# Placing tokens' rows by expert in memory, and gathering the experts' results by token

## The chip, the cores and the metric

The kernel runs on one core of one Trainium2 chip. The metric is the device time of one execution in microseconds (us); kernels are compared by the median of several executions. The engines are called as the profile calls them: PE (matrix multiply; PEld is its weight load), DVE (vector), ACT (activations), POOL (GpSimd, which also issues the indirect DMAs) and SP (which issues the plain DMAs).

## The reference

All data are float32. `x` is 32 x 112 x 256 (batch, time, feature), the context is 32 x 375 x 256. One decoder layer is computed: a delta-rule attention block, a cross-attention with 16 heads over the context, and a mixture of six experts. Only the last matters for the change:

```python
xt = layernorm(x).reshape(-1, 256)
logits = xt @ gate_w.T + gate_b
w, idx = top_k(sigmoid(logits), 2)            # two of six experts for each token
w = w / (w.sum(-1, keepdims=True) + 1e-8)
ge = sum(one_hot(idx, 6) * w[..., None], 1)
y = 0
for e in range(6):
    h = silu(xt @ ew1[e].T) * (xt @ ew3[e].T)
    y = y + ge[:, e:e+1] * (h @ ew2[e].T)
z = (silu(xt @ fc1.T) * (xt @ fc2.T)) @ fc3.T # shared by all tokens
x = x + y + z
```

## The kernel before

The 32 batches are worked in 8 groups of `GB` = 4 batches (448 tokens; a tile is 112 tokens by 4 batches by 256 features, 448 KB). The loop runs over 128 quads of cross-attention work (a batch, half of the heads, and so on) and two slots more. Sixteen slots make one group, about 146 us. The cross-attention of one group is the backbone; into its slots the loop puts pieces of other streams: `main` (the delta block of the next group), `kv` (keys and values of the next batch), and `others` (`mixture_sparse`, the mixture of the group before).

**Order of the work.** A `Recorder` collects all instructions as nodes with modelled prices and dependences, and `flush` writes out the order on PE, DVE and ACT. POOL's and SP's instructions stand in their queues in the order that this plan gives them; each of the two queues then runs in order. All recorded operations carry one line in the profile, L376, but for those written by functions of their own (the experts' matmuls `up` at L1329 and `down` at L1346, the results' scatter at L1357). A DMA's arrival is modelled in the plan, and on the chip each instruction waits by semaphores for what it really needs.

**The mixture.** The tokens of the first seven groups (`SB` = 28 batches, 3136 tokens) are routed sparsely: each token goes to its two experts, 6272 rows in all, done in `NTM` = 54 tiles of `TM` = 128 rows. The last group's tokens pass through all six experts (`mixture_dense`).

- `normed` makes `a3`, the normalised tokens of a group, in a ring of three buffers (tag `h`), which the delta block's tiles use too.
- `dispatch` (L1099) stores `a3` plainly to `rows` by SP, works out with DVE and two small matmuls a place for each token and choice (`row_i`: expert times `CAP` plus the count so far, where `free` holds the next free place of each expert), and issues eight indirect scatters on POOL, one for each batch and choice. Each writes 112 numbers of 4 bytes, the token's number, to that place of one of eight `lists`. The lists are zeroed at the start by eight DMAs on POOL.
- `mixture_sparse` ends by keeping the group's residual and shared part in memory (`kept<-x`).
- `tables` (L1202), in the last group, works out from the counts which expert each tile has (`which`), gathers the eight lists for the 54 tiles by eight indirect gathers, adds and turns them by eight matmuls against the identity (`plist`), and so gets `take` (which row of `rows` each slot of a tile takes) and `put` (where in `results` its result goes; a spare row for an empty slot).
- `gather` and `sparse_tiles` (L1294, L1302) work a pipeline over the tiles: an indirect gather of 128 rows (POOL), a transpose (PE, ACT), `up`, silu and product (ACT, DVE), a transpose, `down`, a copy to `y`, and an indirect scatter of `y` into `results` (POOL).
- `combine` (L1384) runs beside the dense experts of the last group. For each of the seven groups it loads `kept` and the two halves of `results` plainly by SP, into nine borrowed tiles (`homes`, so three groups are in flight), and DVE adds both halves with their gates (56 operations); `store` writes the group out.

At the start SP's queue holds the loads of inputs and weights, then the writes and reads by which the delta block turns its blocks (`blocks<-W`, `C<-blocks`, `X<-blocks`). In a middle group SP's queue holds the loads of context (`cT`) and mask (`mk`), the row store, `kept`, and the load of x two groups ahead.

Of the kernel before, what the change touches and what calls it, by code (L numbers as in the profile page):

```python
# [88 lines left out]
class Recorder:  # L89
# [135 lines left out]

    def together(self, cost):

        rec = self

        class Piece:  # L230
            def __enter__(self):
                rec.whole, rec.held = cost, None

            def __exit__(self, *_):
                rec.whole = rec.held = None

        return Piece()
# [143 lines left out]
def tile_decoder(ctx: ExitStack, tc: tile.TileContext, t: dict, out: bass.AP):  # L381
# [24 lines left out]
    CAP = NL * TM  # L406
# [16 lines left out]

    lists = [dram.tile([NE * CAP, 1], F32, name=f"lists_{i}") for i in range(2 * GB)]
    rows = dram.tile([SB * T, D], F32, name="rows")

    results = dram.tile([2 * SB * T + NTM * TM, D], F32, name="results")
# [19 lines left out]
    while s < T:  # L449
# [27 lines left out]
    zeros = att.tile([TM, NE * NL], F32, tag="neg", name="zeros")  # L477
    nc.vector.memset(zeros, 0.0)
# [9 lines left out]
    )  # L488
    number = const.tile([T, 2, SB], F32, tag="number", name="number")
    nc.gpsimd.iota(  # L490
        number, pattern=[[SB * T, 2], [T, SB]], base=1, channel_multiplier=1, allow_small_or_imprecise_dtypes=True
# [25 lines left out]
    for table in lists:  # L517
        nc.gpsimd.dma_start(out=table.rearrange("(p l) o -> p (l o)", p=TM), in_=zeros)
# [10 lines left out]
    def matmul(dst, lhsT, rhs, start=True, stop=True):  # L529
        n = 1  # L530
        for k in dst.shape[1:]:
            n *= k
        spent[0] += 2 * max(0.125, 0.017 + n / 1200)
        nc.tensor.matmul(dst, lhsT, rhs, start=start, stop=stop)
# [5 lines left out]
    def bank(name):  # L540
        return rec.bank()
# [557 lines left out]
    def dispatch(g, a3, place, ge):  # L1099

        nc.sync.dma_start(
            out=rows[g * GB * T : (g + 1) * GB * T].rearrange("(b t) d -> t b d", t=T), in_=a3
        )
# [23 lines left out]
        for b in range(GB):  # L1127
            for c in range(2):
                i = g * GB + b
                nc.gpsimd.indirect_dma_start(  # L1130
                    out=lists[2 * b + c][:], out_offset=bass.IndirectOffsetOnAxis(ap=row_i[:, c, i : i + 1], axis=0),
                    in_=number[:, c, i : i + 1], in_offset=None,
                )
            if b < GB - 1:
                yield

# [65 lines left out]
    def tables():  # L1202


        def tab(name, shape, dt=F32):
            return late.tile(shape, dt, tag=name, name=name)
# [4 lines left out]
        at = tab("at", [1, NTM])  # L1211
        nc.gpsimd.iota(at, pattern=[[1, NTM]], base=0, channel_multiplier=0, allow_small_or_imprecise_dtypes=True)
        line = tab("line", [NTM, 1])
        nc.gpsimd.iota(line, pattern=[[0, 1]], base=0, channel_multiplier=1, allow_small_or_imprecise_dtypes=True)
# [4 lines left out]
        more = scratch[:, : NE * NL].rearrange("p (e l) -> p e l", l=NL)  # L1219
# [7 lines left out]
        for e in range(1, NE):  # L1227
# [4 lines left out]
        nc.vector.tensor_tensor(d, off[:, 1:], off[:, : NE - 1], ALU.subtract)  # L1232

        past = tab("tpast", [NTM, NE - 1])
        nc.vector.tensor_scalar(past, before_e[:NTM, 1:], line, None, ALU.is_le)
        nc.vector.tensor_tensor(past, past, d[:NTM], ALU.mult)
        src = tab("tsrc", [NTM, 1])
        nc.vector.tensor_reduce(out=src, in_=past, axis=AX.X, op=ALU.add)
        nc.vector.scalar_tensor_tensor(src, src, 1.0 / TM, line, ALU.mult, ALU.add)
        nc.vector.tensor_scalar_min(src, src, float(NE * NL - 1))  # L1240
        srci = tab("tsrci", [NTM, 1], U32)
        nc.vector.tensor_copy(srci, src)

        shape = [1, NTM, NE - 1]
        over = scratch[:1, NE * NL : NE * NL + NTM * (NE - 1)].rearrange("p (i e) -> p i e", e=NE - 1)
        nc.vector.tensor_tensor(
            over, at[:1].unsqueeze(2).to_broadcast(shape), before_e[:1, 1:].unsqueeze(1).to_broadcast(shape), ALU.is_ge
        )
        expert = tab("expert", [1, NTM])
        nc.vector.tensor_reduce(out=expert, in_=over, axis=AX.X, op=ALU.add)  # L1250
        which = tab("which", [1, NTM], I32)
        nc.vector.tensor_copy(which, expert)
        yield
        listed = []
        for i, table in enumerate(lists):
            part = late.tile([NTM, TM], F32, tag=("xg", "xg", "xg", "xg", "xT", "xT", "hs", "hs")[i],
                             name=f"listed_{i}", bufs=4 if i < 4 else 2 if i < 6 else 3)
            nc.gpsimd.indirect_dma_start(
                out=part, out_offset=None, in_=table.rearrange("(l p) o -> l (p o)", p=TM),
                in_offset=bass.IndirectOffsetOnAxis(ap=srci, axis=0),  # L1260
            )
            listed.append(part)
            if i % 2 == 1:
                yield
        pt = bank("plist")
        for i, part in enumerate(listed):
            matmul(
                pt[:, :NTM], part, ident[:NTM, :NTM], start=(i == 0), stop=(i == len(listed) - 1)
            )
        num = tab("num", [P, NTM])  # L1270
        nc.vector.tensor_scalar_add(num, pt[:, :NTM], -1.0)
        taken = tab("ttaken", [P, NTM])
        nc.vector.tensor_scalar(taken, num, 0.0, None, ALU.is_ge)
        second = tab("tsecond", [P, NTM])
        nc.vector.tensor_scalar(second, num, float(SB * T), -float(SB * T), ALU.is_ge, ALU.mult)
        nc.vector.tensor_tensor(second, second, num, ALU.add)
        nc.vector.tensor_scalar_max(second, second, 0.0)
        take = tab("take", [P, NTM], U32)
        nc.vector.tensor_copy(take, second)
        spare = tab("spare", [P, NTM])  # L1280
        nc.gpsimd.iota(
            spare, pattern=[[TM, NTM]], base=2 * SB * T, channel_multiplier=1, allow_small_or_imprecise_dtypes=True
        )
        nc.vector.tensor_tensor(num, num, spare, ALU.subtract)
        nc.vector.tensor_tensor(num, num, taken, ALU.mult)
        nc.vector.tensor_tensor(num, num, spare, ALU.add)
        put = tab("put", [P, NTM], U32)
        nc.vector.tensor_copy(put, num)
# [3 lines left out]
        yield from sparse_tiles(take, put, which, gathers)  # L1292
# [9 lines left out]
    def sparse_tiles(take, put, which, xgs):  # L1302
# [4 lines left out]
        xTs, hs, hTs, at, scatters = {}, {}, {}, {}, []  # L1307
# [33 lines left out]
        def down(i):  # L1341
            p, hT = bank("pw2"), hTs[i]

            def issue():
                for c in range(CH):
                    rec.nc.tensor.matmul(  # L1346
                        p[:, :D].real(), hT[:, c, :], w2[:, bass.ds(at[i] * (CH * D) + c * D, D)],
                        start=(c == 0), stop=(c == CH - 1),
                    )

            rec.add("tensor", "down", [p], [hT, ew2], (issue, (), {}), cost=1.0)
            spent[0] += 1.0
            y = late.tile([TM, D], F32, tag="y", name=f"y_{i}", bufs=3)
            nc.vector.tensor_copy(y, p[:, :D])

            def scatter():
                sent = rec.nc.gpsimd.indirect_dma_start(  # L1357
                    out=results[:], out_offset=bass.IndirectOffsetOnAxis(ap=put[:, i : i + 1], axis=0),
                    in_=y, in_offset=None,
                )  # L1360
                for other in scatters:
                    tc.declare_no_dep(sent.ins, other.ins, reason="they write different rows")
                scatters.append(sent)

            rec.add(
                "gpsimd", "indirect_dma_start", [results[:]], [y, put[:, i : i + 1]], (scatter, (), {}), loose=True
            )
# [16 lines left out]
    def combine():  # L1384
# [7 lines left out]
        def ask(g):  # L1392
            three = []
            for i in range(3):
                h = homes[(3 * g + i) % len(homes)]
                if i == 0:
                    src = kept[g].rearrange("b t d -> t b d")
                else:
                    at = ((i - 1) * SB + g * GB) * T
                    src = results[at : at + GB * T].rearrange("(b t) d -> t b d", t=T)  # L1400
                nc.sync.dma_start(out=h, in_=src)
                three.append(h)
            return three
# [70 lines left out]
    for n in range(len(quads) + 2):  # L1474
# [29 lines left out]
        if last:  # L1504
            mains.append(main)
            side += [others] * ((0, 0, 0, 1, 1, 1, 2, 1, 1, 1, 1, 0, 0, 0, 0, 0)[i] if g < groups else 0)
            side += [tiles] * ((0, 0, 0, 0, 0, 0, 0, 1, 1, 1, 1, 1, 3, 4, 4, 4)[i] if g < groups else 3)
        else:
            if g > 0 and i in (3, 4, 5, 7, 8, 9, 10, 11, 12):
                side.append(others)  # L1510
            if i == 13 and g + 2 < groups:
                x_of[g + 2] = load_x(g + 2)
                following = ahead(g + 2)
# [116 lines left out]
```

## Time and profile before

| what | value |
|---|---|
| median of 17 runs | 1458.04 us (1453.1 to 1463.65) |
| profiled execution, its time | 1454.55 us |
| its span | 1452.9 us, 26668 instructions |
| granted PE clock, mean | 0.972 |
| DMA | 73.13 MB in 77170 packets, 29864 of them under 512 B |
| HBM | read 51.12 MB, written 20.28 MB |

Profile times are microseconds from the span's start. A line of the timeline gives start, duration, engine, line, operation, what is written from what is read, and in brackets the idle time of the engine before it and what ended it; "issue" is a wait that the profile does not explain, "remote" one that it cannot place. SPq is SP's DMA queue.

The work by time: startup to about 100 us, the middle to about 1140 (seven groups), tables and lists to 1196, the tile phase to T0 = 1380.1, the dense experts with `combine` to the end.

```profile
PE   6679999999999899999999999999989889999998
DMA  8100100101010101010101020102015111222283
...
L376 POOL DMA_INDIRECT lists<-number,row_i x56 | 52.8, 944 | 110.5 <-DVE tn L376 57.0
L376 POOL DMA_INDIRECT xg<-rows,take x54 | 52.5, 972 | 73.2 <-PE bank L376 56.2
...
L1357 POOL DMA_INDIRECT results<-y,put x54 | 53.2, 985 | 39.6 <-DVE y L376 20.1
```

The first two rows are busy tenths in 40 slices of the span (PE, DMA engines). The others give count, busy time, mean ns of one and idle time before.

### The profile page before, as it was taken

Reading aid. Unit: us, or ns where it says so; the run is one execution under the profiler, and the core shown is the slowest. Engines: PE = TensorE matmul, PEld = TensorE weight load, DVE = VectorE, ACT = ScalarE, POOL = GpSimd, SP = SyncE. Lnnn points to the kernel's source line nnn. Section 1 sums busy time; section 2 is a strip of 40 time slices with the busy share of each in tenths; the row PEclk is TensorE's granted clock in tenths of the full one; section 3 lists DMA queues with packets and bytes.
Section 4 is the critical chain, followed back from the end, with each engine's and each line's share of the span. In section 5 each row is a group of like instructions: output and inputs, shape, how many; then the busy total and the mean of one; then the engine's idle time right before and its main releaser. Section 6 shows DMA issues by size and latency. Waiting matters only on the chain.

```text
span 1452.9 us, 26668 instructions
## 1 busy us (share of the span) xinstructions
PE 1376.8 (95%) x9716; PEld 932.5 (64%) x9716; DVE 965.0 (66%) x3164; ACT 701.3 (48%) x1946; POOL 319.7 (22%) x492
## 2 busy tenths in 40 slices
PE   6679999999999899999999999999989889999998
PEld 4456766766676567766766676667656565656655
DVE  6545766866785578667857786778548555455577
ACT  2123756654665356546655555456548364222110
POOL 3122000320032003200320032003200314556500
PEclk9779999999999999999999999999999889999999
DMA  8100100101010101010101020102015111222283
GB/s 232 26 7 13 34 16 17 48 17 42 17 48 16 42 16 48 17 42 16 48 17 42 16 49 16 42 16 59 6 48 154 20 43 58 90 82 88 68 234 101
DMA packets 77170, 73.13 MB, mean 50 GB/s; under 512 B 29864, under 2 KB 72808, under 8 KB 77040
## 3 DMA queue, kind: packets, MB, share of 16 engines
q1 hardware_dynamic: 69296, 56.00, 14.1%
q0 software_dynamic: 7744, 15.43, 3.6%
q8 instruction: 77, 1.26, 0.4%
q14 instruction: 53, 0.43, 0.1%
HBM read 51.12 MB, written 20.28 MB: 49 GB/s over the span
## 4 chain that ended last, share of the span: by engine, by line
PE 74%; DVE 11%; ACT 4%; issue 3%; DMA 2%; POOL 2%; another core or an unknown queue 1%; DVEq 0%; SPq 0%; ACTq 0%
PE bank L376 64%; PE bank L1329 7%; PE bank L1346 3%; ACT e L376 2%; POOL W L376 2%; DVE e L376 2%; DVE rs_u L376 2%; DVE x L376 1%; DMA blocks<-W 1%; DVE W L376 1%; ACT eT L376 1%; DVE rs_i L376 1%; DVE vx L376 1%; DMA X<-blocks 1%
## 5 line engine op out<-in xcount | busy, mean ns | idle before, releaser
L376 ACT ACTIVATE e<-e,nmx 112x375 f32<-112x375 f32 x512 | 306.2, 603 | 172.4 <-DVE nmx L376 169.7
L376 DVE CUSTOM_DVE_ANT_0 e<-bank,neg,flip 112x375 f32<-112x375 f32 x512 | 282.4, 604 | 42.1 <-PE bank L376 29.7
L376 ACT COPY eT<-bank 125x448 f32<-125x448 f32 x384 | 184.9, 530 | 117.8 <-PE bank L376 78.4
L376 PEld LDWEIGHTS bank<-ident,e 112*125 112x125 f32 x1536 | 187.4, 189 | 39.9 <-issue 15.6
L376 PE MATMUL bank<-ident,e 112*125 112x112 f32 x1536 | 205.0, 277 | 7.8 <-issue 3.0
L376 PE MATMUL bank<-kx,qz 32*112 32x375 f32 x1024 | 125.8, 526 | 0.0
L376 PE MATMUL bank<-eT,vx 125*32 125x112 f32 x3072 | 105.0, 265 | 17.6 <-ACT eT L376 10.5
L376 PEld LDWEIGHTS bank<-eT,vx 125*32 125x32 f32 x3072 | 70.3, 110 | 70.3 <-issue 46.9
L1329 PE MATMUL bank<-ew,xT 128*128 x216 | 104.0, 605 | 2.4 <-ACT xT L376 2.3
L376 PE MATMUL bank<-w_xwvT,cT 128*125 128x256 f32 x384 | 104.2, 399 | 0.0
L376 PE MATMUL bank<-cT,w_xwkT 128*128 128x375 f32 x256 | 96.4, 502 | 2.5 <-ACT eT L376 2.5
L376 ACT ACTIVATION_READ_ACCUMULATOR e<-e,nmx 112x1 f32 x512 | 97.8, 191 | 0.0
L376 DVE SCALAR_TENSOR_TENSOR hs<-hs,bank 128x256 f32<-128x256 f32 x108 | 45.4, 421 | 77.2 <-ACT hs L376 65.0
L376 DVE SCALAR_TENSOR_TENSOR qk<-qk,bank 128x448 f32<-128x448 f32 x56 | 34.8, 621 | 81.7 <-ACT qk L376 54.2
L376 ACT ACTIVATE hs<-bank 128x256 f32<-128x256 f32 x54 | 20.7, 384 | 119.5 <-PE bank L1329 99.1
L376 PEld LDWEIGHTS bank<-w_xwvT,cT 128*125 128x125 f32 x384 | 68.3, 191 | 14.0 <-issue 6.0
L376 POOL DMA_INDIRECT lists<-number,row_i x56 | 52.8, 944 | 110.5 <-DVE tn L376 57.0
L376 PEld LDWEIGHTS bank<-kx,qz 32*112 32x112 f32 x1024 | 44.0, 172 | 41.1 <-issue 13.3
L376 PEld LDWEIGHTS bank<-cT,w_xwkT 128*128 128x128 f32 x256 | 44.9, 193 | 38.1 <-issue 9.8
L376 POOL DMA_INDIRECT xg<-rows,take x54 | 52.5, 972 | 73.2 <-PE bank L376 56.2
L376 POOL TENSOR_TENSOR u<-h,nwb 112x1024 f32<-112x1024 f32 x7 | 16.6, 2370 | 232.3 <-issue 218.8
L1357 POOL DMA_INDIRECT results<-y,put x54 | 53.2, 985 | 39.6 <-DVE y L376 20.1
(251 smaller groups left out, 2394.0 us busy)
## 6 DMA issues: line engine op xcount, KB each, us to landing
cT<-in_ctxT_dram SPq DMA_DIRECT2D x32, 375.0 KB
mk<-in_mask_dram SPq DMA_DIRECT2D x32, 164.1 KB
x<-in_x_dram SPq DMA_DIRECT2D x7, 448.0 KB
rows<-h SPq DMA_DIRECT2D x7, 448.0 KB
kept<-x SPq DMA_DIRECT2D x7, 448.0 KB
e<-results SPq DMA_DIRECT2D x6, 448.0 KB
eT<-results SPq DMA_DIRECT2D x4, 448.0 KB
out_dram<-x SPq DMA_DIRECT2D x4, 448.0 KB
```

The source lines that it names most:

```text
L376: getattr(getattr(self.nc, name), op)(*[real(a) for a in args], **{k: real(v) for k, v in kwargs.items()})
L1329: rec.nc.tensor.matmul(p.real(), xT[:, c, :], w13[:, bass.ds(at[i] * (NC * 2 * MI) + c * 2 * MI, 2 * MI)], start=(c == 0), stop=(c == NC - 1),
L1346: rec.nc.tensor.matmul(p[:, :D].real(), hT[:, c, :], w2[:, bass.ds(at[i] * (CH * D) + c * D, D)], start=(c == 0), stop=(c == CH - 1),)
L1357: sent = rec.nc.gpsimd.indirect_dma_start(out=results[:], out_offset=bass.IndirectOffsetOnAxis(ap=put[:, i : i + 1], axis=0), in_=y, in_of ...
```

## The change

`rows` becomes a memory of `NE * CAP` rows by expert and place (`CAP` is now 3136, as many as there are tokens), with one row of zeros after the last. `dispatch` no longer stores `a3` plainly. It scatters the rows of `a3` themselves (112 rows of 1 KB) to their two places, eight indirect DMAs on POOL for each group as before. The lists, the numbers and the lists' zeroing are gone. Places that may stay empty must hold zeros: the loop issues `clear_places(g, e)` on SP, one store of 448 KB of zeros from `blank` for each of the first seven groups and six experts (42 in all), in slots 8 to 13 of a group; a clear covers the places of expert e that lie from g*448 on. `hold` ties the node just recorded to the last PE node before it, which is the plan's means of keeping clears and scatters near the place where they are recorded. In SP's queue of the changed program the clears stand in seven places: seven of them near the start (behind the loads of weights and a mask, ahead of a context and of `blocks<-W` and `C<-blocks`), six in each of five middle groups (ahead of `cT`, `kept<-x`, `mk` and `x<-in_x_dram`), and five beside the last scatters. In the middle groups their waits interleave with the scatters: two scatters, clears, two scatters, and so on.

`tables` computes `take` by DVE from the counts alone (tile times 128 plus place, shifted by each expert's offset, and the row of zeros where a tile ends beyond its expert's tokens), with no list gathers and no matmuls, and rewrites `row_i` to say where in `results` each token's two results lie. `sparse_tiles` stores each `y` plainly by SP, 128 KB a tile, to its own 128 rows of `results`. `combine` gets both halves by eight indirect gathers of 112 rows for each group on POOL, 56 in all; `kept` is still loaded by SP. The first piece of `tables` is asked for in slot 10 of the last group, before in slot 7.

In the order of the last group's POOL queue stand now: eight scatters, 54 gathers of rows, 56 gathers of results.

```diff
+    def hold(self):
+
+        so_far = next(node for node in reversed(self.nodes) if node.eng == "PE")
+        self.nodes[-1].before[so_far.at] = so_far
...
-    CAP = NL * TM
+    CAP = SB * T
...
-    lists = [dram.tile([NE * CAP, 1], F32, name=f"lists_{i}") for i in range(2 * GB)]
-    rows = dram.tile([SB * T, D], F32, name="rows")
-    results = dram.tile([2 * SB * T + NTM * TM, D], F32, name="results")
+    ZERO = NE * CAP
+    rows = dram.tile([ZERO + 1, D], F32, name="rows")
+    results = dram.tile([NTM * TM, D], F32, name="results")
+    blank = const.tile([T, D], F32, tag="blank", name="blank")
+    nc.vector.memset(blank, 0.0)
...
-    for table in lists:
-        nc.gpsimd.dma_start(out=table.rearrange("(p l) o -> p (l o)", p=TM), in_=zeros)
+    nc.gpsimd.dma_start(out=rows[ZERO : ZERO + 1], in_=blank[:1])
...
     def dispatch(g, a3, place, ge):
-        nc.sync.dma_start(
-            out=rows[g * GB * T : (g + 1) * GB * T].rearrange("(b t) d -> t b d", t=T), in_=a3
-        )
...
-                i = g * GB + b
-                nc.gpsimd.indirect_dma_start(
-                    out=lists[2 * b + c][:], out_offset=bass.IndirectOffsetOnAxis(ap=row_i[:, c, i : i + 1], axis=0),
-                    in_=number[:, c, i : i + 1], in_offset=None,
-                )
+                place_row(g * GB + b, c, a3[:, b, :])
...
+    def clear_places(g, e):
+        some = rows[e * CAP + g * GB * T : e * CAP + (g + 1) * GB * T]
+        nc.sync.dma_start(
+            out=some.rearrange("(t r) d -> t r d", t=T), in_=blank.unsqueeze(1).to_broadcast([T, GB, D])
+        )
+        rec.hold()
+    placed = []
+    def place_row(i, c, row):
+        where = row_i[:, c, i : i + 1]
+        def scatter():
+            sent = rec.nc.gpsimd.indirect_dma_start(
+                out=rows[:], out_offset=bass.IndirectOffsetOnAxis(ap=where, axis=0), in_=row, in_offset=None
+            )
+            for other in placed:
+                tc.declare_no_dep(sent.ins, other.ins, reason="they write different rows")
+            placed.append(sent)
+        rec.add("gpsimd", "indirect_dma_start", [rows[:]], [row, where], (scatter, (), {}), loose=True)
+        rec.hold()
...
-        listed = []
-        for i, table in enumerate(lists):
...
-            nc.gpsimd.indirect_dma_start(
-                out=part, out_offset=None, in_=table.rearrange("(l p) o -> l (p o)", p=TM),
-                in_offset=bass.IndirectOffsetOnAxis(ap=srci, axis=0),
-            )
...
-        pt = bank("plist")
-        for i, part in enumerate(listed):
-            matmul(
-                pt[:, :NTM], part, ident[:NTM, :NTM], start=(i == 0), stop=(i == len(listed) - 1)
-            )
...
+            nc.vector.tensor_tensor(moved, flat if e == 1 else moved, past, ALU.subtract)
+        nc.vector.tensor_copy(row_i.rearrange("t c b -> t (c b)"), moved)
+        yield from sparse_tiles(take, which, gathers)
...
-            def scatter():
-                sent = rec.nc.gpsimd.indirect_dma_start(
-                    out=results[:], out_offset=bass.IndirectOffsetOnAxis(ap=put[:, i : i + 1], axis=0),
-                    in_=y, in_offset=None,
-                )
...
+            nc.sync.dma_start(out=results[i * TM : (i + 1) * TM], in_=y)
...
                 if i == 0:
-                    src = kept[g].rearrange("b t d -> t b d")
+                    nc.sync.dma_start(out=h, in_=kept[g].rearrange("b t d -> t b d"))
                 else:
-                    at = ((i - 1) * SB + g * GB) * T
-                    src = results[at : at + GB * T].rearrange("(b t) d -> t b d", t=T)
-                nc.sync.dma_start(out=h, in_=src)
+                    for b in range(GB):
+                        where = row_i[:, i - 1, g * GB + b : g * GB + b + 1]
+                        nc.gpsimd.indirect_dma_start(
+                            out=h[:, b, :], out_offset=None, in_=results[:],
+                            in_offset=bass.IndirectOffsetOnAxis(ap=where, axis=0),
+                        )
...
-            side += [tiles] * ((0, 0, 0, 0, 0, 0, 0, 1, 1, 1, 1, 1, 3, 4, 4, 4)[i] if g < groups else 3)
+            side += [tiles] * ((0, 0, 0, 0, 0, 0, 0, 0, 0, 0, 1, 2, 4, 4, 4, 4)[i] if g < groups else 3)
         else:
...
+            if 8 <= i < 8 + NE:
+                clear_places(g, i - 8)
```

More of the change, by code (lines that the diff above doesn't have):

```diff
@@ L476, in tile_decoder @@
     nc.vector.memset(ones, 1.0)
-    zeros = att.tile([TM, NE * NL], F32, tag="neg", name="zeros")
-    nc.vector.memset(zeros, 0.0)
     nothing = moe.at("hT", 0, [P, t["fc3T"].shape[0] // P, NT])
@@ L487, in tile_decoder @@
         channel_multiplier=0,
-    )
-    number = const.tile([T, 2, SB], F32, tag="number", name="number")
-    nc.gpsimd.iota(
-        number, pattern=[[SB * T, 2], [T, SB]], base=1, channel_multiplier=1, allow_small_or_imprecise_dtypes=True
     )
@@ L1210, in tables @@
         scratches.append(scratch)
-        at = tab("at", [1, NTM])
+        at = tab("at", [P, NTM])
         nc.gpsimd.iota(at, pattern=[[1, NTM]], base=0, channel_multiplier=0, allow_small_or_imprecise_dtypes=True)
-        line = tab("line", [NTM, 1])
-        nc.gpsimd.iota(line, pattern=[[0, 1]], base=0, channel_multiplier=1, allow_small_or_imprecise_dtypes=True)
+        row = tab("trow", [P, NTM])
+        nc.gpsimd.iota(row, pattern=[[TM, NTM]], base=0, channel_multiplier=1, allow_small_or_imprecise_dtypes=True)
         step = tab("tstep", [P, NL])
@@ L1218, in tables @@
         nc.vector.tensor_tensor(n, free, head, ALU.subtract)
-        more = scratch[:, : NE * NL].rearrange("p (e l) -> p e l", l=NL)
+        shape = [P, NTM, NE - 1]
+        size = NTM * (NE - 1)
+        more = scratch[:, 2 * size : 2 * size + NE * NL].rearrange("p (e l) -> p e l", l=NL)
         nc.vector.tensor_tensor(
@@ L1232, in tables @@
         nc.vector.tensor_tensor(d, off[:, 1:], off[:, : NE - 1], ALU.subtract)
[L1234 to L1247, printed above, removed]
-        )
-        expert = tab("expert", [1, NTM])
+        ends = tab("tends", [P, NE - 1])
+        nc.vector.tensor_tensor(ends, free[:, 1:], free[:, : NE - 1], ALU.subtract)
@@ L1250, in tables @@
+        over = scratch[:, :size].rearrange("p (i e) -> p i e", e=NE - 1)
+        part = scratch[:, size : 2 * size].rearrange("p (i e) -> p i e", e=NE - 1)
+        spread = lambda v: v.unsqueeze(1).to_broadcast(shape)
+        nc.vector.tensor_tensor(over, at.unsqueeze(2).to_broadcast(shape), spread(before_e[:, 1:]), ALU.is_ge)
+        expert = tab("expert", [P, NTM])
         nc.vector.tensor_reduce(out=expert, in_=over, axis=AX.X, op=ALU.add)
-        which = tab("which", [1, NTM], I32)
+        which = tab("which", [P, NTM], I32)
@@ L1252, in tables @@
         nc.vector.tensor_copy(which, expert)
-        yield
-        listed = []
-        for i, table in enumerate(lists):
-            part = late.tile([NTM, TM], F32, tag=("xg", "xg", "xg", "xg", "xT", "xT", "hs", "hs")[i],
-                             name=f"listed_{i}", bufs=4 if i < 4 else 2 if i < 6 else 3)
-            nc.gpsimd.indirect_dma_start(
-                out=part, out_offset=None, in_=table.rearrange("(l p) o -> l (p o)", p=TM),
-                in_offset=bass.IndirectOffsetOnAxis(ap=srci, axis=0),
-            )
-            listed.append(part)
-            if i % 2 == 1:
-                yield
@@ L1265, in tables @@
-        pt = bank("plist")
-        for i, part in enumerate(listed):
-            matmul(
-                pt[:, :NTM], part, ident[:NTM, :NTM], start=(i == 0), stop=(i == len(listed) - 1)
[L1269 to L1285, printed above, removed]
@@ L1286, in tables @@
-        nc.vector.tensor_tensor(num, num, spare, ALU.add)
-        put = tab("put", [P, NTM], U32)
-        nc.vector.tensor_copy(put, num)
+        added = tab("tadded", [P, NTM])
+        nc.vector.tensor_tensor(part, over, spread(d), ALU.mult)
+        nc.vector.tensor_reduce(out=added, in_=part, axis=AX.X, op=ALU.add)
+        nc.vector.tensor_tensor(row, row, added, ALU.add)
+        nc.vector.tensor_tensor(part, over, spread(ends), ALU.mult)
+        nc.vector.tensor_reduce(out=added, in_=part, axis=AX.X, op=ALU.add)
@@ L1289, in tables @@
+        nc.vector.tensor_scalar(added, added, free[:, 0:1], None, ALU.add)
+        nc.vector.tensor_tensor(added, row, added, ALU.is_lt)
+        nc.vector.tensor_scalar_add(row, row, -float(ZERO))
+        nc.vector.tensor_tensor(row, row, added, ALU.mult)
+        nc.vector.tensor_scalar_add(row, row, float(ZERO))
+        take = tab("take", [P, NTM], U32)
+        nc.vector.tensor_copy(take, row)
+        yield
         for _ in range(4):
@@ L1291, in tables @@
         yield
-        yield from sparse_tiles(take, put, which, gathers)
+        flat = row_f.rearrange("t c b -> t (c b)")
+        moved = scratch[:T, : 2 * SB]
+        for e in range(1, NE):
+            past = scratch[:T, 2 * SB * e : 2 * SB * (e + 1)]
+            nc.vector.tensor_scalar(past, flat, head[:T, e : e + 1], d[:T, e - 1 : e], ALU.is_ge, ALU.mult)
+            nc.vector.tensor_tensor(moved, flat if e == 1 else moved, past, ALU.subtract)
+        nc.vector.tensor_copy(row_i.rearrange("t c b -> t (c b)"), moved)
+        yield from sparse_tiles(take, which, gathers)
     def gather(i, take):
@@ L1300, in gather, with sparse_tiles @@
         return xg
-    def sparse_tiles(take, put, which, xgs):
+    def sparse_tiles(take, which, xgs):
         w13 = ew13.rearrange("p e c j n -> p (e c j n)")
@@ L1306, in sparse_tiles @@
         CH = MI // P
-        xTs, hs, hTs, at, scatters = {}, {}, {}, {}, []
+        xTs, hs, hTs, at = {}, {}, {}, {}
         def turn(src, tag, pool, name, n, on_act):
@@ L1354, in down @@
             nc.vector.tensor_copy(y, p[:, :D])
-            def scatter():
-                sent = rec.nc.gpsimd.indirect_dma_start(
-                    out=results[:], out_offset=bass.IndirectOffsetOnAxis(ap=put[:, i : i + 1], axis=0),
-                    in_=y, in_offset=None,
[L1360 to L1367, printed above, removed]
+            nc.sync.dma_start(out=results[i * TM : (i + 1) * TM], in_=y)
         for k in range(NTM + 4):
```

## The prediction

> **What bounds the kernel now.** I read the page's busy times and chain first, then the windows by stage, then the timeline of each place that the diff touches.
>
> ```profile
> PE 1376.8 (95%) x9716; PEld 932.5 (64%) x9716; DVE 965.0 (66%) x3164; ACT 701.3 (48%) x1946; POOL 319.7 (22%) x492
> PE 74%; DVE 11%; ACT 4%; issue 3%; DMA 2%; POOL 2%; another core or an unknown queue 1%; DVEq 0%; SPq 0%; ACTq 0%
> ```
>
> PE sets the time. Of the span's 1452.9 us it idles 76, and this change adds or removes little matmul work, so it counts only where it fills or lengthens those 76. The windows (start:end, length, then busy PE, PEld, DVE, ACT, POOL, clock, DMA share, GB/s) say where they lie:
>
> ```profile
> 100.00:1000.00 900.00, 881.16 (x6927) 607.02 (x6926) 639.27 (x2161) 518.32 (x1444) 164.11 (x307) 0.99 0.11 30
> 1150.00:1167.00 17.00, 6.98 (x39) 3.66 (x35) 3.63 (x11) 1.32 (x4) 10.17 (x11) 0.60 0.23 14
> 1200.00:1380.00 180.00, 179.16 (x824) 111.66 (x824) 93.09 (x259) 45.82 (x136) 99.90 (x102) 0.99 0.24 78
> 1380.00:1453.00 73.00, 66.90 (x225) 40.67 (x223) 53.18 (x123) 7.62 (x14) 1.00 (x1) 0.98 0.61 167
> ```
>
> The middle and the tile phase are nearly full. One hole stands out, 10 us of idle PE at 1150 (and a clock of 0.60 for what it does there), beside the list scatters and list gathers that the change removes:
>
> ```profile
> 1152.24 0.93 POOL L376 DMA_INDIRECT lists<-number,row_i  x1 [0.30 <-issue]
> 1153.48 0.98 POOL L376 DMA_INDIRECT xg<-lists,tsrci  x1 [0.31 <-issue]
> 1160.55 0.38 PE L376 MATMUL bank<-eT,vx 125*32 125x112 f32 x1 [1.02 <-issue]
> 1166.36 0.53 ACT L376 COPY eT<-bank 125x448 f32<-125x448 f32 x1 [15.68 <-remote]
> ```
>
> PE's matmuls come one per 0.71 to 1.4 us, with no wait on any tensor ("issue"), while ACT stands 15.7 us. The work done there takes 3 to 4 us at the usual rate, so the hole costs about 13.
>
> **Startup.** Seven clears of 448 KB enter SP's queue ahead of C's load (before: W out at 34.51, C at 37.54, C used at 52.3). A 448 KB transfer moves in about 2.05 us (the closing stores), so C lands some 14 us later, at 52 to 54: 0 to 2 us late on the delta chain, which is a latency chain there (PE busy 78 of the first 110 us). Against it, eight zeroing stores on POOL (600 KB, 6 to 17 us) go, worth 0 to 2. I take +1, bounds -2 to +5.
>
> **Middle groups.** Before, eight 4-byte scatters (944 ns + 0.30) run at 317.4 to 327.2 and repeat in each group. POOL is next needed at 365:
>
> ```profile
> 365.24 2.36 POOL L376 TENSOR_TENSOR u<-h,nwb 112x1024 f32<-112x1024 f32 x1 [38.03 <-issue]
> 347.25 0.33 SPq L376 DMA_DIRECT2D x<-in_x_dram  x1
> 351.60 0.43 DVE L376 BATCH_NORM_STATS2 bst<-x 112x6 f32<-112x256 f32 x1 [0.58 <-DMA x<-in_x_dram]
> ```
>
> The new scatters issue at the same price (row gathers of the same shape: 972 ns + 0.30). But `hold` puts them between clears in program order, and both write `rows`, so clear and scatter wait for each other: s0 s1, two clears, s2 s3, one, s4 s5, one, s6 s7, two. No such pair is in the trace; I build it from a scatter's 2.45 us from issue to landing (last result scatter 1380.94, its reader issued 1383.39), a plain 448 KB transfer's 3.4 (343.87 to 347.25) and 2.05 for a second behind it. From 317 that ends at 343 to 350. On POOL, u, C and W stand behind it, needed at 365: covered, by 15 us at least. The tile the scatters read is next written by DVE at 371: covered. The row store that goes would have been hidden too. On SP, cT, kept, mk and x stand behind the clears; SP was free for cT at 340.23 and becomes free at 346 to 350. cT and mk have 15 us or more, but x has none: DVE already waits 0.58 us on it. x lands 6 to 7 us later, DVE's new order reaches it some 4 us later, so DVE stalls 3 to 4 in each of five groups. DVE is 66% busy and PE has queued work, so of that PE loses between nothing and 2.4: 0 to +12, taken at 1 us each, +5. The extra 18.8 MB of zeros add about 42 x 2.05 = 86 us of moving at a DMA share that now averages 0.11 in the middle: hidden, otherwise inside these bounds.
>
> **Tables and tiles.** The eight list matmuls go (1186.2 to 1188.1 on PE): -2. DVE's wider tables add about 4 us, eight gathers less make room: 0. The first tile's wait on ACT xT (2.3 us, 1196.4 to 1198.7) should shrink as tables finish earlier: -1.5 (0 to -2.3). In the tile phase a tile takes PE 3.02 us; its 128 KB store on SP instead of a scatter of 985 ns on POOL lies beside it either way: 0.
>
> **Tail.** Before, after the last down-projection (T0 = 1380.1) the results are loaded plainly and PE's dense experts set the end:
>
> ```profile
> 1380.94 1.00 POOL L1357 DMA_INDIRECT results<-y,put  x1 [1.36 <-DVE y L376]
> 1383.39 0.84 SPq L376 DMA_DIRECT2D e<-results  x2
> 1447.85 0.69 DVE L376 TENSOR_TENSOR x<-x,bank 112x512 f32<-112x512 f32 x1 [1.04 <-PE bank L376]
> ```
>
> That is T0 + 72.8 to 1452.9. After, 56 gathers by token stand in POOL's queue, the first waiting for every results store: copy 0.55 and a 128 KB store of 2.1 to 2.3, so T0 + 2.9. Gathers run every 1.26 us (xg gathers 1192.22, 1193.50, 1194.77, 1196.02), 55 intervals 69.3; issue to use is 3.15 (1192.22 to 1195.37). The last data are there at T0 + 75.4. What is queued on DVE behind the last two combines is a hidden product, two fc3 blocks of PE (1.8 each, partly beside), two adds of 0.69 and the store with the end, 4.4: T0 + 83.9. POOL's gathers take the place of PE's 68 us of dense work as the bound: **+11**, bounds +9 (faster gathers, DVE's tail beside them) to +13.
> The Trainium skill, "DMA: Bandwidth & Descriptors", in its anatomy of the GpSimd path, gives such a transfer a fixed cost of about 2.0 us; were that paid in series, 56 would take 112 us and the tail would be an estimated 41 us worse still. The spacing of 1.26 speaks against it, as successive gathers overlap.
>
> **Sum.** Against the profiled run (1454.55; span and 1.65 around it, 3.5 below the median of the 17 runs): +1 +5 -2 -1.5 +11 = +13.5 before stalls. The hole at 1150 then decides. Instruction blocks of 16 KB land in 0.95 us as a rule, but in 2.9 to 3.6 just behind the 4-byte list scatters at six sites, and in 0.9 to 1.3 beside 1 KB row gathers and scatters. So I believe the hole belongs to 4-byte traffic and goes: -13, total +0.5. If not at all, 0.
> The same page, under its specifications, says that transfers under 512 B make the DMA engine read, modify and write; by it all such traffic of the dispatch goes, and the sum would be that of the first rival below. The block loads agree with its direction; no row shows the mechanism.
>
> **The rivals.**
> *All stalls were the lists' (0.23).* ACT also stands "remote" 8.2 us at 476.9 and 8.8 at 1051, each about 17 us behind the start of a group's scatters; PE idles 5.4 and 5.1. If those go as well: +0.5 - 10.5 = -10, 1448. For: the place. Against: four sites of six show none, and both begin 8 us after the last scatter.
> *The hole comes back (0.37).* Eight scatters are still issued at 1143 to 1153, now of 1 KB rows, between 448 KB clears, and instruction blocks took 1.75 us beside such bursts. ACT stops at 1150.7, before the first list gather, so scatters alone may start it. If blocks of PE and ACT that fall there still come late, the 13 are not gained: +13.5, 1471.5. It decides as soon as less than 10 of the 13 go. It would also appear at another site of the seven, since block borders move with the program.
> *The tail is covered after all:* if DVE reached the gathered groups as they come and PE's 68 us still ended last, tail 0 and total -10.5. The order on DVE, combines ahead of the last hidden products, speaks against; I count this within the first rival's share.
>
> **How the numbers follow.** My forecast, hole gone and other stalls staying, has 0.40: 1458.04 + 0.5 = 1458.5. Its terms spread it by about 7 either way, 1452 to 1466. A measurement of this kernel tells about 0.2% (2.9 us) from no change; of the 0.40, 0.10 lies faster than that, 0.15 within, 0.15 slower. With the rivals: faster 0.23 + 0.10 = 0.33, same 0.15, slower 0.37 + 0.15 = 0.52. The range takes in the first rival's 1448 less 4 and the second's 1471.5 plus 3.5: 1444 to 1475, which leaves out about 0.18.
>
> **What would show it.** Right: no stretch of one matmul per 0.7 us near 1150 and ACT's 15.7 us gone; POOL one gather per 1.26 us for 70 us to within 9 us of the end, PE idle in the last 15; SP free at 346 to 350 in a group, x landing near 358. Wrong: matmuls on "issue" again at scatters or clears (second rival); POOL's u released late by scatters, or a clear that waits longer than 2.45 us for its pair, in which case the middle costs more than 12; gathers further apart than 1.3 us.

## The result, and the profile after

The changed kernel takes 1493.4 us (median of 8 runs, 1492.51 to 1498.61) against 1457.18 (median of 46): a ratio of 1.0256, 95% interval 1.0241 to 1.0270. It is slower by 36 us; 1458.5 had been forecast, with 1475 as the upper end. Its profiled execution has a span of 1492.2 us, 39.3 above that of before.

The page's row of busy times and the windows of the changed kernel (columns as before), cut at the events that the two kernels share: the first dispatch (317), the last dispatch (1156), the tile phase, the end of the last down-projection (1376).

```profile
PE 1383.8 (93%) x9700; PEld 935.8 (63%) x9700; DVE 966.2 (65%) x3171; ACT 701.5 (47%) x1946; POOL 305.2 (20%) x477
317.00:1156.00 839.00, 813.69 (x6394) 560.39 (x6393) 582.34 (x1981) 473.43 (x1315) 142.02 (x245) 0.99 0.20 58
1156.00:1200.00 44.00, 38.65 (x306) 25.39 (x305) 28.56 (x106) 25.61 (x75) 13.29 (x14) 0.96 0.21 61
1200.00:1376.00 176.00, 176.00 (x862) 111.85 (x860) 94.35 (x267) 48.31 (x144) 45.72 (x48) 1.00 0.25 79
1376.00:1492.00 116.00, 75.11 (x226) 44.37 (x224) 53.51 (x122) 7.49 (x14) 51.82 (x56) 0.81 0.36 104
```

PE works as much as before (1383.8 against 1376.8). The hole at the last dispatch is smaller (PE idles 5 of the 44 us behind it, before 10), the tile phase is full, and the last stretch is 116 us long with PE at work for only 75 of it. Between the same events the two profiles compare so:

| stretch | before | after | difference | forecast |
|---|---|---|---|---|
| start to first dispatch | 317.4 | 317.5 | 0.0 | +1 |
| to last dispatch | 826.0 | 838.9 | +12.9 | +5 |
| to last down-projection | 236.6 | 219.8 | -16.8 | -16.5 |
| to the end | 72.8 | 116.0 | +43.2 | +11 |

So the start came as worked out, and the second and the last row did not. The third agrees in its sum, but not because the hole went. The eight row scatters of the last dispatch run back to back (POOL, 1156.4 to 1166.0), and just behind them stand:

```profile
1165.70 0.26 PE L381 MATMUL bank<-eT,vx 125*32 125x112 f32 x1 [0.46 <-issue]
1167.11 0.39 PE L381 MATMUL bank<-eT,vx 125*32 125x112 f32 x3 [1.15 <-issue]
1167.87 0.69 DVE L381 TENSOR_TENSOR x<-x,bank 112x512 f32<-112x512 f32 x1 [5.50 <-remote]
1168.16 0.53 ACT L381 COPY eT<-bank 125x448 f32<-125x448 f32 x1 [3.27 <-remote]
```

PE's matmuls come one by one on "issue" again, which the prediction had named as the sign of its second rival. What is left of the hole costs some 8 us, as a chip without it shows further below.

The timeline of the tail, each line from its engine's own list (start, duration, engine, operation, idle time before it and what ended it):

```profile
1384.39 0.92 POOL L381 DMA_INDIRECT e<-results,row_i  x1 [0.30 <-ACT hT L381]
1399.27 0.54 ACT L381 ACTIVATE hT<-bank 128x448 f32<-128x448 f32 x1 [14.95 <-remote]
1409.77 0.62 DVE L381 SCALAR_TENSOR_TENSOR hT<-hT,bank 128x448 f32<-128x448 f32 x1 [8.91 <-remote]
1410.44 5.23 PE L381 MATMUL bank<-ew,hT 128*112 128x256 f32 x14 [16.13 <-issue]
1450.10 0.54 ACT L381 ACTIVATE hT<-bank 128x448 f32<-128x448 f32 x1 [18.83 <-remote]
1457.88 0.92 POOL L381 DMA_INDIRECT e<-results,row_i  x1 [0.30 <-issue]
```

Gathers are 1.23 us apart from 1379.5 on, as forecast, with the last issued at 1457.9 (three gaps of 2 to 8 us are POOL's waits for DVE). But beside them ACT, DVE and PE stand for 5 to 21 us at a time. Where the engines' order lets one follow it, what they need was there: ACT's product at 1399.27 reads a bank that PE filled by 1391, DVE's at 1409.77 one that PE had filled by 1392 and its own tile of 1400.5. None of the long idle stretches ends on gathered data; over the whole kernel DVE waits 1.1 us for it.

A middle group, from the timeline and DVE's waits (us in total, times, longest; `bst` is the first work on x):

```profile
326.88 0.93 POOL L1144 DMA_INDIRECT rows<-h,row_i  x1 [7.10 <-DMA rows<-blank]
321.38 26.74 SPq L381 DMA_DIRECT2D rows<-blank  x6
355.70 0.33 SPq L381 DMA_DIRECT2D x<-in_x_dram  x1
358.96 0.43 DVE L381 BATCH_NORM_STATS2 bst<-x 112x6 f32<-112x256 f32 x1 [3.18 <-DMA x<-in_x_dram]
DVE bst L381 <- DMA x<-in_x_dram: 22.4, 5, 5.8
```

Scatters and clears wait for each other in turn as built on paper: SP is held from 321.4 to 348.1 (346 to 350 forecast), and x is asked for 8.5 us later than before (6 to 7 forecast).

### The profile page after: what moved, and what is told of

The parts are those of the page before. It is cut to its first block, busy times and chain, and to the rows that moved or that the text cites. A ratio compares the mean times of both kernels' runs of the same rounds, so it can differ in the third digit from the quotient of the medians.

```text
span 1492.2 us, 26826 instructions
## 1 busy us (share of the span) xinstructions
PE 1383.8 (93%) x9700; PEld 935.8 (63%) x9700; DVE 966.2 (65%) x3171; ACT 701.5 (47%) x1946; POOL 305.2 (20%) x477
## 3 DMA queue, kind: packets, MB, share of 16 engines
q8 instruction: 77, 1.26, 0.3%
## 5 line engine op out<-in xcount | busy, mean ns | idle before, releaser
L381 PE MATMUL bank<-ident,e 112*125 112x112 f32 x1536 | 208.7, 279 | 9.4 <-DVE nmx L381 5.6
L1144 POOL DMA_INDIRECT rows<-h,row_i x56 | 52.5, 938 | 223.7 <-DMA rows<-blank 118.6
L381 DVE SCALAR_TENSOR_TENSOR hT<-hT,bank 128x448 f32<-128x448 f32 x56 | 34.6, 618 | 52.2 <-issue 18.8
L381 ACT ACTIVATE hT<-bank 128x448 f32<-128x448 f32 x28 | 14.9, 537 | 102.9 <-remote 46.3
```

Source lines behind the costliest of these rows:

```text
L381: getattr(getattr(self.nc, name), op)(*[real(a) for a in args], **{k: real(v) for k, v in kwargs.items()})
L1144: sent = rec.nc.gpsimd.indirect_dma_start(out=rows[:], out_offset=bass.IndirectOffsetOnAxis(ap=where, axis=0), in_=row, in_offset=None)
```

## The experiments

Two theories stood at first. **A**: GpSimd's (POOL's) stream of gathers costs the tail its 43 us, and in one form (**A1**) it does so by stopping the other engines, whatever the data. Its rival (**A2**): DVE waits in order for gathered data and the others for DVE, or the changed order is late by itself. For the middle, **C1**: x is late because SP stands in the clears' waits; rival **C2**: the writes themselves slow the middle. The runs fell on several chips, and this turned out to matter: on one of them (chip 9) the kernel before takes 1456 us, on the others (1, 5, 6, 7) 1428 to 1431. "Tail" is the time from the end of the last down-projection to the end of the span.

**The tail without gathers (chip 6).**

```diff
-                    for b in range(GB):
-                        where = row_i[:, i - 1, g * GB + b : g * GB + b + 1]
-                        nc.gpsimd.indirect_dma_start(out=h[:, b, :], ...)
+                    at = ((i - 1) * SB + g * GB) * T
+                    nc.sync.dma_start(out=h, in_=results[at : at + GB * T].rearrange(...))
```

> The changed kernel, with the 56 gathers by token at the end replaced by plain loads of the same tiles by SP (it leaves out finding each token's own results; the rest is kept). The changed kernel's last down-projection ends at 1376 and its span at 1492, 116 us later, where the kernel before needed 73. Theory A (the stream of gathers costs the tail its 43 us): the tail is again 72 to 75 us, the time about 1450. Rival B (the tail is long because something else of the changed order is late, DVE's or PE's order): the tail stays over 90 us, the time above 1468.

Measured: 1437.88 us, against 1429.01 for the kernel before on this chip, ratio 1.0076 (1.0049 to 1.0103). The tail is 71.7 us. Theory A holds as far as that: with plain loads the changed order has before's tail. But with the kernel before at 1429 here, not 1457, the absolute times of the expectation had lost their footing.

**Gathers that nobody reads (chip 6).** As above, and in addition:

```diff
+                    for b in range(GB):
+                        xg = late.tile([TM, D], F32, tag="xg", name=f"idle_{g}_{i}_{b}", bufs=4)
+                        where = row_i[:, i - 1, g * GB + b : g * GB + b + 1]
+                        nc.gpsimd.indirect_dma_start(out=xg[:T, :256], in_=results[:], ...)   # offsets: where
```

> As the kernel with the plain tail, but the 56 gathers are issued all the same, into a small ring that nobody reads. Theory A1 (a back-to-back stream of GpSimd's indirect transfers stops the other engines, whatever the data): ACT, DVE and PE show idle stretches of 5 to 15 us with no tensor waited for while the stream runs, and the tail is 95 to 115 us, the time 1472 to 1492. Rival A2 (DVE waits in order for gathered data, and the others for DVE): no such stretch, PE's dense work ends 68 us after the last down-projection, the gathers end beside it or some 7 us later, the time 1450 to 1460.

Measured: 1447.17, ratio 1.0128 (1.0111 to 1.0145), tail 77.9, and no idle stretch of the kind. PE's work ends 66.8 us into the tail, as without gathers; POOL's last gather ends 5.7 us behind that, and the span follows it. A2's numbers, on this chip: A1 seemed refuted.

**Clears behind the load of x (chip 6).**

```diff
-            if 8 <= i < 8 + NE:
-                clear_places(g, i - 8)
             if i == 13 and g + 2 < groups:
                 x_of[g + 2] = load_x(g + 2)
                 following = ahead(g + 2)
+            if i == 14:
+                nc.vector.memset(blank, 0.0)
+                rec.hold()
+                for e in range(NE):
+                    clear_places(g, e)
```

> The changed kernel, with a group's six clears held back (by a write of the zeros on DVE in slot 14) until after the load of x two groups ahead. Theory C1 (x lands late because SP stands before it in the clears' waits; DVE waited 4.5 us for x in each of five groups and PE lost that): DVE's wait on x falls from 22 us to under 4, the time falls by 15 to 23, to 1470 to 1478. Rival C2 (the clears' writes themselves slow the middle): the wait on x may go, but the time stays within 5 us of the changed kernel's 1493.

Measured: 1423.0, ratio to the kernel before 0.9961 (0.9945 to 0.9977): the changed idea with this one edit is 0.4% faster than before on this chip. SP's queue and the window of the middle (318.2 to 1124.8 from first to last dispatch):

```profile
348.07 0.33 SPq L381 DMA_DIRECT2D x<-in_x_dram  x1
363.45 7.30 SPq L381 DMA_DIRECT2D rows<-blank  x6
DVE bst L381 <- DMA x<-in_x_dram: 2.1, 3, 1.1
318.00:1124.00 806.00, 796.91 (x6393) 552.81 (x6392) 573.65 (x1983) 474.69 (x1313) 142.03 (x245) 1.00 0.21 61
```

The same 42 clears are written, all of a group's in one run after x. The wait on x falls to 2.1 us, and from the first to the last dispatch the middle takes 806.6 us, against 833.5 in the run with plain loads at the end, whose clears stand early on the same chip. C1 holds and C2 falls: the same bytes, written later, cost little, so it is their place that costs. That it is x alone isn't separated: the edit moves the clears behind all loads of a group, and lets its eight scatters run back to back.

**List scatters held apart in the kernel before (chip 6).**

```diff
+                pace = small.tile([T, 1], F32, tag="pace", name=f"pace_{i}_{c}", bufs=1)
+                nc.gpsimd.tensor_copy(pace, number[:, c, i : i + 1])
                 nc.gpsimd.indirect_dma_start(
                     out=lists[2 * b + c][:], ...
-                    in_=number[:, c, i : i + 1], in_offset=None,
+                    in_=pace, in_offset=None,
```

> The kernel before, with its eight list scatters of a group held apart: each takes its numbers from one small tile that is copied after the scatter before it has landed. The eight list gathers stay back to back. Theory A1 (back-to-back transfers stop the other engines, 4 bytes or 1 KB alike): ACT's 8 us stops at 477 and 1051 go (PE lost 10.5 there), the hole at 1150 shrinks from 13 to about 7, the time falls by 10 to 18. Rival D (4-byte writes do it, however spaced): the stops stay, the time stays within 4 us. Third possibility: the 12 us longer scatters delay the tables and the first tile, and cost up to 10.

Measured: 1464.09, ratio 1.0230 (1.0202 to 1.0259). The third possibility came, far larger than I gave it:

```profile
326.21 0.18 POOL L376 COPY pace<-number 112x1 f32<-112x1 f32 x1 [4.38 <-DMA lists<-pace,row_i]
374.46 2.34 POOL L376 TENSOR_TENSOR u<-h,nwb 112x1024 f32<-112x1024 f32 x1
```

A 4-byte list scatter, with no other under way, took 4.6 to 9.6 us until it had landed (eight of the first dispatch, median 5.6; I had used 2.45, from the results' 1 KB rows), so eight one after the other took 54 us, past the point where POOL's `u` is needed (365 before); the tables came late too. The run says nothing about the stops, since this chip may have none. It does say one thing by the way: instruction blocks of 16 KB took 2.7 to 3.6 us beside its 4-byte scatters, as in the first profile, and no engine stopped on that account.

**The same kernels on chip 9.** The kernel before was profiled here as well.

> The kernel before, unchanged, for its profile beside the other runs of this call. In the first profile ACT stood 8 to 16 us at three places and PE lost 24 us there, and the time was 1458; beside the four experiments its median was 1429. Theory E (the stops are a property of the chip or session that ran it): where the time is near 1429 the profile has no such stops; where it is near 1458 it has them at the same places. Rival: the time differs for another reason (clock, memory), and the stops are there in both.

> The changed kernel, unchanged. Theory E: where the kernel before shows no stops, the tail is what the gathers' spacing gives, 83 us from the last down-projection and not 116, and the clears still cost the middle 20 to 23; the time is 1446 to 1452, 1.2 to 1.6% above the kernel before. Where the kernel before has its stops, 2.4 to 2.7% above, as first measured. Rival: the ratio is 1.0256 on every chip.

> The version with clears held behind the load of x, once more beside the changed kernel. Without stops: 1421 to 1425, 25 us below the changed kernel and 0.2 to 0.6% below the kernel before. With stops: 20 to 27 below the changed kernel, and still above the kernel before by 5 to 15.

> Gathers that nobody reads, again. Where the kernel before shows its stops: 5 to 15 us idle stretches on ACT, DVE and PE during the stream, tail above 95 us (theory A1: the stream itself stops the engines). Where it doesn't: tail 78 to 80 us and no such stretch, as in the run before.

The kernel before took 1456.38 here (median of 7) and shows its stops at the same places (ACT 8.9, 8.5 and 15.7 us). The changed kernel took 1495.23, ratio 1.0264 (1.0242 to 1.0285), tail 117.1. Late clears took 1464.63: 30.6 below the changed kernel, and 1.0053 (1.0037 to 1.0070) of the kernel before; their tail is 117.0. The gathers that nobody reads took 1509.86, with a tail of 130.6. That profile beside the one of chip 6, ACT and PE around the end of the stream, and the windows of the stream, chip 9 first:

```profile
1449.27 0.92 POOL L381 DMA_INDIRECT xg<-results,row_i  x1 [0.30 <-issue]
1454.62 1.20 PE L381 MATMUL bank<-ew,hT 128*112 128x256 f32 x2 [49.51 <-DVE hT L381]
1459.55 0.54 ACT L381 ACTIVATE hT<-bank 128x448 f32<-128x448 f32 x1 [58.26 <-remote]
1378.00:1460.00 82.00, 27.43 (x85) 15.34 (x83) 11.75 (x28) 3.17 (x6) 51.79 (x56) 0.70 0.29 85
```

```profile
1364.00:1440.00 76.00, 66.57 (x225) 40.85 (x223) 31.86 (x66) 7.60 (x14) 51.62 (x56) 0.95 0.33 99
```

One program, two chips, the gathers' spacing the same (1.23 us), read by nobody: on chip 9 ACT stands 58 us and PE 50 (PE behind DVE, which stands too and does two pieces of work in between), and they go on 5 us (PE) and 10 us (ACT) after the last gather's start; on chip 6 nothing stops. This is A1, but not on every chip. Three rivals can be read off these two profiles. The plain loads are not it: no plain transfer runs on chip 9 from 1384 to the end of the stops. Nor are slower transfers: the gathers' packets take 0.13 us on the average on both chips. Nor is the granted clock: it is still 1.00 from 1398 to 1409, while ACT, after 1401, and PE, after 1405, already stand, and falls to half only behind that. The changed order with plain loads alone was not run on chip 9; the nearest is the kernel before, whose tail, with plain loads, is 72.7 us there. The first profiles show the same stops, so they likely came from a chip of this kind.

**What of the stream does it (chips 5, 7 and 1).** Four variants of the idle gathers: rows of 256 bytes (`d=64`), 16 rows instead of 112 (`row_i[:16, ...]`), only the 28 of one choice (`if i == 1`), and those 28 with indices copied into one of two small tiles, so that at most two gathers are under way.

> The kernel with the plain tail and 56 gathers that nobody reads, each of 112 rows of 256 bytes in place of 1 KB. Where gathers of 1 KB stopped the engines, the tail was 131 us (ACT stood 58 us). Theory F1 (the number of row descriptors or of transfers does it, not the bytes): the stops are as long, the tail 120 to 135. Rival F2 (the bytes crowd out something): the stops shrink to a quarter, the tail is 80 to 95. On a chip without stops: 78 to 80.

> The same 56 gathers that nobody reads, each of 16 rows of 1 KB in place of 112. Theory F3 (each row's descriptors on GpSimd's queue do it): the stops shrink to under 10 us, the tail is 73 to 90. Rival F4 (each transfer instruction does it, however small): stops over 25 us, the tail over 100. On a chip without stops: 73 to 80.

> 28 gathers of 112 rows of 1 KB that nobody reads, back to back (some 35 us). Theory A1: the engines stop for the stream's length and some 8 us behind it, 25 to 40 us in all, the tail 95 to 110. Rival: stops come only beyond a backlog of more than 28, the tail 73 to 78. On a chip without stops: 73 to 75.

> The same 28 gathers, but each takes its indices from one of two small tiles that GpSimd copies only when the gather before the last has landed, so at most two are under way and the stream lasts 45 to 60 us. Theory A1 with backlog (the stop needs a dense stream; the scatters held in pairs in the middle of the changed kernel showed none): no stop over 3 us, the tail 73 to 78. Rival (each gather costs the others the same, paced or not): stops as with 28 back to back, the tail 95 to 110. On a chip without stops: 73 to 75.

All four, one execution each, fell on a chip without stops (5): tails of 77.9, 72.4, 71.8 and 71.7 us. Three were run again, on chip 7:

> 56 gathers of 16 rows of 1 KB that nobody reads, back to back. On a chip with stops, where 112 rows gave a tail of 131 us: theory F3 (rows' descriptors do it) stops under 10 us, tail 73 to 90; rival F4 (each transfer does it, however small) stops over 25 us, tail over 100. On a chip without stops the tail is 78, as in the run before.

> 28 gathers of 112 rows of 1 KB that nobody reads, back to back. On a chip with stops: theory A1 (the engines stand for the stream's length and some 8 us behind it) tail 95 to 110; rival (only a longer backlog does it) tail 73 to 78. On a chip without stops: 74 to 76.

> The same 28 gathers, at most two under way. On a chip with stops: theory A1 with a dense stream as its condition, no stop over 3 us and a tail of 73 to 78; rival (each gather costs the same, paced or not) a tail of 95 to 110. On a chip without stops: 74 to 76.

Again no stops: tails of 73.7, 71.8 and 71.8. What in the stream makes a chip stop stays open. A pair of runs on chip 9 bears on it: with late clears a group's eight row scatters go out back to back, and DVE stood 3.8 us at each of the first six dispatches; in the changed kernel, where they are held in pairs, it did so only once, for 2.7. At the seventh both have eight back to back, and DVE stood 5.4 in both. With late clears on chip 6 it stood at none. That is a hint that dense streams do it; pacing the gathers on such a chip wasn't measured.

**The changed kernel where nothing stops (chip 1).**

> The changed kernel, unchanged. On a chip where the kernel before takes 1425 to 1431 (no stops): the tail is 82 to 85 us, as forecast, the middle as late as before, and the time 1446 to 1452, 1.2 to 1.6% above the kernel before. Where the kernel before takes 1452 to 1460: 2.4 to 2.8% above. Rival: 2.5% on every chip.

> 28 gathers that nobody reads, back to back. With stops: a tail of 95 to 110 us if the engines stand for the stream's length, 73 to 78 if only a longer backlog stops them. Without stops: 74 to 76.

> The same 28 gathers, at most two under way. With stops: a tail of 73 to 78 if a dense stream is needed for a stop, 95 to 110 if each gather costs the same. Without stops: 74 to 76.

The changed kernel took 1449.16 against 1429.99, ratio 1.0134 (1.0113 to 1.0155). The two variants had tails of 71.7 and 71.8. The windows from its last dispatch on and of its last stretch, its last gather and DVE's waits:

```profile
1155.00:1200.00 45.00, 43.78 (x362) 28.02 (x361) 34.30 (x123) 27.94 (x83) 16.16 (x17) 1.00 0.25 72
1367.00:1450.00 83.00, 69.95 (x228) 42.01 (x226) 54.56 (x123) 7.84 (x15) 52.44 (x56) 0.97 0.50 146
1439.25 0.92 POOL L381 DMA_INDIRECT e<-results,row_i  x1 [0.30 <-DVE x L381]
DVE bst L381 <- DMA x<-in_x_dram: 23.3, 5, 5.5
```

The tail is 82.7 us (83.9 had been worked out) against 71.7 with plain loads: the gathers as a bound cost 11.0 us, the forecast's +11. The wait on x is the same as on chip 9 (22.6). From the last dispatch to the last down-projection this kernel takes 211.9 us, as every changed version does on chips 1, 5, 6 and 7 (211.8 to 212.1); on chip 9 it takes 220.7, and in the first profile it took 219.8. So the two places where the changed kernel stops make up the difference between the chips: 34.4 us in the tail and 8.8 here, of 41.9 between the two spans.

## Why the prediction was wrong, point by point

**The tail's +11 is the step that failed most.** Its parts were right: the start (the first gather 3.2 us after the last down-projection, 2.9 forecast), the spacing (1.23 against 1.26), the drain at the end; where nothing stops it measured +11.0. It took the gathers for a bound on POOL with the other engines free beside it. What it left out is that on the measured chip the stream stops these engines: +43, of which some 34 are stops (tails of 117.1 us on chip 9 and 82.7 on chip 1). The sign was in the profile of before. I read the hole of 1150 as a price of 4-byte traffic and took its removal as a gain, and did not ask what 56 more indirect transfers back to back would do, when 16 of them had stopped ACT for 15.7 us. They move 1 KB rows, and I had told these to be harmless from their spaced use in the tile phase.

**The hole went only in part, and that the sum fits is luck.** The stretch behind the last dispatch gave -16.8 against -16.5 forecast, but 8 to 9 us of it are still stops, just behind eight scatters of 1 KB rows: the second rival's sign, with more than half of its 13 us. So taking out the lists' work must have been worth more than the 3.5 us taken for it. How much isn't shown, as the kernel before wasn't profiled where nothing stops; with the hole at 13, an estimate is 236.6 - 13 - 211.9 = 11.7.

The reason given for the hole fails too. 4 bytes are not needed for a stop: rows of 1 KB that nobody reads stop ACT for 58 us. And slow instruction blocks, my evidence, weren't there: the block that the profile of before shows at the hole (1151.4) landed in 0.93 us, the slow ones stand at other dispatches (five of 16 KB, where I had counted six), and chip 6 has them without a stop. The Trainium skill, "Runtime: NRT & Kernel Launch", under "Instruction fetch mechanics", has the fetch of the next block mostly hidden; the blocks recorded during the idle gathers' stream took 0.3 to 0.7 us on chip 9 and 0.5 to 1.0 on chip 6, so the records agree with it and give no late block as the cause. What was removed is eight indirect gathers right behind eight scatters: ACT stood 15.7 us there, and 3.3 (DVE 5.5) behind the eight scatters alone. ACT's two stops of 8 us, at dispatches that are now held in pairs, went too, as the first rival had it (-10.5).

**The middle was mis-sized.** I took x to be 6 to 7 us late and DVE to stand 3 to 4 us in each of five groups, and measured 8.5 and 4.5 (22.4 in five). The error is the next factor: I priced PE's loss at 1 us a group because DVE is 66% busy and PE has work queued. Between the first six dispatches a group takes 147.0 us on chip 9 in the changed kernel and 140.5 with late clears: 6.5 each. So the cost of DVE's wait was not absorbed by PE's queued work, as I had assumed; that it runs on through a chain that PE needs a few microseconds later is likely, but no run shows it by itself. From the first to the last dispatch, early clears cost 837.1 - 808.4 = 28.7 us on chip 9 (the sixth interval is 3.6 shorter with them). In the first profiles, against the kernel before, only +12.9 is seen, because ACT's stops went in the same stretch.

**Startup** (+1 forecast): 0.0. **Tables and tiles** (-3.5 forecast): not measured apart from the hole, as said above. The rivals' shares did not help: I had one rival in which stops stay and one in which all go, and none in which they move to the tail and grow.

## What to carry to other kernels

An engine that stands with no tensor to wait for, beside a dense run of another engine's transfers, is a price of that run until shown otherwise; before adding more of the same, find what in it does the harm, and take the longest stop seen as the price. A clear or other cheap store is not free where it stands: put it behind the loads that the next stage waits for, which here was worth 30.6 us with the same bytes written. And a transfer that is due in the middle of a chain is priced by the whole chain behind it, not by the waiting engine's idle share.

Late clears are the best version found: 0.4% faster than the kernel before where nothing stops (0.9961), 0.5% slower (1.0053) where the stream of gathers still costs its stops (a tail of 117.0 us).

## What the runs showed of the hardware that I had not expected

The same program differed by chip (or by a state of the chip that these runs can't tell from it) in how GpSimd's indirect transfers weigh on the other engines. The kernel before, with eight or sixteen in a row, took 1456 us on chip 9 and 1428 to 1431 on chips 1, 5, 6 and 7; a row of 56 made a tail of 130.6 us on chip 9 and 77.9 on chip 6. What the stopped engines wait for is in no record of these traces, and stays open. The kernel before wasn't profiled on a chip without stops, so that its 27 us there are the stops is likely (its three stops of ACT cost PE some 24) but not shown.

An indirect scatter of 112 numbers of 4 bytes took 4.6 to 9.6 us until the next instruction could see it landed (median 5.6 of eight); one of 128 rows of 1 KB, 2.45. And the issue of a gather hardly depends on its size: 0.92 us for 112 rows of 1 KB or of 256 bytes, 0.84 for 16 rows.
